# A recurrent gate on one core: the first weight pair's low-rank part ahead of everything, and block 1 spread over more engines

## The chip, the cores and the metric

The kernel runs on one core of a Trainium2 chip. The metric is device time in microseconds. The core has five engines with queues of their own, each worked off in order: TensorE (PE, matmul), VectorE (DVE), ScalarE (ACT), GpSimd (POOL), and SyncE (SP), which here only issues DMAs.

## The reference, cut to what matters

The input is x, 2 x 1024 tokens of 512 features. With xn the layer norm of x, the output is x + s * silu(f). Here f is a gated feed-forward net with low-rank (LoRA) additions, and s is a long convolution whose kernel comes from a small state space model:

```
def _lora_linear(x, w, a, b):
    base = jnp.einsum('bsd,od->bso', x, w)
    low = jnp.einsum('bsr,or->bso', jnp.einsum('bsd,rd->bsr', x, a), b)
    return base + low * SCALING            # SCALING = 2, rank R = 16
h1 = _lora_linear(x, w1, lora_A1, lora_B1)     # 512 -> 1376
h3 = _lora_linear(x, w3, lora_A3, lora_B3)
g = jax.nn.silu(h1) * h3
return _lora_linear(g, w2, lora_A2, lora_B2)   # 1376 -> 512

K = _s4_kernel(Lambda, p, q, B, Ct, step, L)   # L = 512
y = irfft(rfft(u, n=2*L) * rfft(K, n=2*L), n=2*L)[..., :L] + D[0] * u
```

All is float32.

## The kernel before, in words

**Tokens.** The 2048 tokens are four blocks of 512 (`x_in[0]` to `x_in[3]`), each four tiles of 128. Blocks 0 and 1 form the first half of the tokens, 2 and 3 the second. Every tile is normalized: its mean and variance come from VectorE's statistics (`norm_stats`, L246 and L247) or from two accumulating ScalarE passes (`act_sums`, `act_squares`, with GpSimd's `act_means` and `act_variances` behind them). `norm_root` (L280 to L283) turns the variances of a block, or of two, into scale and shift by ten tiny VectorE operations, and `normalize` scales the tiles on ScalarE (L292) and GpSimd (L296). `transpose` has TensorE turn a tile (L303) into one of two PSUM banks, and ScalarE copies it out: block 0 and 2 into `xr` (L311), block 1 and 3 into `b12` and `xr` (L313, L314).

**Weights.** The 1376 hidden features are five pairs of 2 x 128 and a last chunk of 96. A pair's tile `w` has eight slots; w1 and w3, cut in half along the 512 features, fill slots 1 (a11), 2 (a12), 0 (a21) and 3 (a22). The low-rank part is not applied to the tokens but added to the weights: `lora_product` (L381) multiplies the rank-16 factors `lo_d` and `lo_h` into a PSUM bank, and `merge` (L391) has VectorE add twice that onto the loaded weights. `merge_pair` does it for pair 0 in two halves, `merge_whole_pair` for the others, `merge_last` for the last chunk.

**Products.** The feed-forward products are two nested seven-product (Strassen-Winograd) schemes. The outer one works on halves of the features and of the tokens, the inner one on the halves within. So there are sums of tokens (`outer_token_sum` L327, `inner_token_sum` L339 to L345) and of weights (`outer_weight_sums` L439, `inner_weight_sum` L451, `last_sums` L490 to L493 on GpSimd), all additions of whole tiles, most of them on VectorE. A `Chain` is one outer product: seven inner products into the banks x, w and y (L754), with copies by ScalarE (L774 takes a snapshot of x, L792 copies x into the bank w, onto which the next product then adds) and additions by VectorE (L778) that gather them. GpSimd multiplies the gated halves (L835) and adds others (L868).

**Order.** The order on each engine is written by hand. `at(place, what)` puts a piece of work on a heap; the pieces are taken out by place, one unit being roughly one product on TensorE, and each engine executes its instructions in that order. The start (loads, norms of block 0, the last chunk's LoRA) comes ahead of the heap as plain code; the places -11 to 0 are the rest of the ramp; the first heavy products start at -11 (last chunk) and -4 (pair 0).

**Start.** SP issues the loads of x blocks 0 and 1, the last chunk, pair 0, x blocks 2 and 3, and pair 1. ScalarE's queue issues the first LoRA factors. TensorE executes products of the identity with itself (`keep_warm`, L989) until there is work.

**Second half.** From about 285 us on the down projection runs in units of 128 tokens (`unit`), together with the state space model's resolvent, roots and matrix (`s4_work`, L561 to L745), a few small VectorE steps after every turn of a unit. `run` takes one turn of a unit, one of a list of `parts` (the sums of the next group's activations, L1176), and some S4 steps, and so on. `nothing` is an empty part.

Of the kernel before, what the change touches and what calls it, by code (L numbers as in the profile page):

```python
# [107 lines left out]
def s4_gated_ffn(  # L108
# [141 lines left out]
    def act_sums(b, tt):  # L250
        if tt == 0:
            sums_of_x[b] = small.tile([P, 3, NTT], F32, tag="act_sums", name="act_sums")
# [4 lines left out]
    def act_means(b):  # L257
        sums = sums_of_x[b]
        nc.gpsimd.tensor_scalar(sums[:, 1, :], sums[:, 0, :], -1.0 / DIM, None, mult)
        nc.gpsimd.tensor_scalar(norms[b][:, :, 0], sums[:, 0, :], 1.0 / DIM, None, mult)  # L260
# [11 lines left out]
    def act_variances(b):  # L272
        nc.gpsimd.tensor_scalar(
            norms[b][:, :, 1], sums_of_x[b][:, 2, :], 1.0 / DIM, None, mult
        )
# [11 lines left out]
    def normalize(b, on_act=(0, 2)):  # L287
        rstd, shift = norms[b]
        for tt, t in enumerate(x_in[b]):
# [5 lines left out]
            else:  # L295
                nc.gpsimd.tensor_scalar(t, t, rstd[:, one], shift[:, one], mult, add)  # L296

    def transpose(b, tiles, tag="aux"):
        sb, low = divmod(b, 2)
        for tt in tiles:  # L300
# [11 lines left out]
            else:  # L312
                nc.scalar.copy(b12[sb][:, :, at_], halves[:, 0])  # L313
# [80 lines left out]
    def load_pair(c):  # L394
        w = wpool.tile([P, 8, 2, 2, P], F32, tag="w", name="w")
        for v, src in enumerate((w1T, w3T)):
            for half in range(2):
                slot = (1, 2, 0, 3)[2 * v + half]
                rows = src[half * HALF : (half + 1) * HALF, PAIR_AT[c] : PAIR_AT[c] + 2 * P]
                nc.sync.dma_start(  # L400
                    out=w[:, slot].rearrange("p k m h -> p k (m h)"),
                    in_=rows.rearrange("(k p) h -> p k h", p=P),
                )
        return w

    def merge_pair(c, w, half, tag="aux"):

        ps = [bank(tag), bank(tag)]
# [4 lines left out]
        for v in range(2):  # L413
            to = w[:, (1, 2, 0, 3)[2 * v + half]].rearrange("p k m h -> p (k m h)")
            after(1.6 + v, lambda to=to, v=v: merge(to, ps[v]))
# [559 lines left out]
    w_pair, s_pair = {0: load_pair(0)}, {c: {} for c in range(NPAIR)}  # L975
# [22 lines left out]
    primed = bank("w"), bank("w")  # L998
    for ps in primed:
        keep_warm(ps, 12, True)  # L1000
    ps_last = lora_last()
    mv = norm_tile(0)
    norm_stats(0, range(NTT))
    norm_root(mv, 0)
    normalize(0)

    for i in range(2):
        keep_warm(primed[1], (5, 2)[i])
        transpose(0, range(2 * i, 2 * i + 2))
# [3 lines left out]
    norm_stats(1, range(2, NTT))  # L1013
    norm_root(mv, 1)
    merge_last(w_last, ps_last, 1)
# [41 lines left out]
    at(-10, lambda: normalize(1))  # L1057
    at(-9.9, lambda: last_sums(w_last, s_last))
    at(-9, lambda: merge_pair(0, w_pair[0], 0))
    at(-3.8, lambda: merge_pair(0, w_pair[0], 1))  # L1060
    for i in range(2):
        at(-6 + i, lambda i=i: transpose(1, range(2 * i, 2 * i + 2), "y"))
# [529 lines left out]
```

## Time and profile before

| | us |
|---|---|
| median of 3 runs | 445.49 (444.50 to 445.88) |
| the profiled execution | 446.04 |
| its span, first to last instruction | 444.2 |
| PE busy | 437.1 |
| VectorE busy | 318.0 |
| GpSimd busy | 206.1 |
| ScalarE busy | 144.6 |

A line of a timeline gives the start and the length in us, engine, source line, operation, output <- inputs, the shape, the number of instructions, and in brackets idle time ahead and what ended it. A chain of waits is followed back from the last instruction, at each step to what released it. DMA share is the mean busy share of the 16 DMA engines.

### The profile page before, as it was taken

The page shows a single profiled execution, that of the slowest core. Times are in us where ns is not written, and L with a number is a line of the kernel's source. Part 1 is how long each engine was busy: PE and PEld are TensorE (multiplying, and loading weights), DVE is VectorE, ACT ScalarE, POOL GpSimd, SP SyncE. Part 2 cuts the span into 40 slices and gives each one's busy share as a digit, 9 for nine tenths or more (in the row PEclk, how much of TensorE's full clock was granted, in tenths as well). Part 3 has the DMA queues.
Part 4 walks back from the last instruction along what each step waited for, and adds up shares of the span by engine and source line. Part 5 has one row for each costly group of instructions (what it writes and reads, how often), then busy time and mean ns, then how long its engine had stood idle before and what let it go on. Part 6 is the DMA issues. An engine that isn't in the chain of part 4 may idle for free.

```text
span 444.2 us, 5192 instructions
## 1 busy us (share of the span) xinstructions
PE 437.1 (98%) x1722; PEld 271.8 (61%) x1722; DVE 318.0 (72%) x534; ACT 144.6 (33%) x296; POOL 206.1 (46%) x156
## 2 busy tenths in 40 slices
PE   8999999999999999999999999999999999999996
PEld 8645333344444444444443447888888999999995
DVE  5799999955984687468745796979595885653234
ACT  2676332543254325532453242111101212212221
POOL 2306469895669467945794469400000122222221
PEclk9999999999999999999999999999999999999999
DMA  8911304025102500260036526395901843323211
GB/s 263 364 51 38 136 0 147 0 76 174 37 24 72 165 24 24 76 180 25 24 123 209 163 91 213 106 357 187 346 19 72 281 141 96 142 95 96 78 65 48
DMA packets 35466, 53.61 MB, mean 121 GB/s; under 512 B 4688, under 2 KB 21520, under 8 KB 35312
## 3 DMA queue, kind: packets, MB, share of 16 engines
q1 hardware_dynamic: 35312, 53.14, 36.6%
q8 instruction: 13, 0.21, 0.2%
q10 hardware_dynamic: 128, 0.14, 0.1%
q14 instruction: 13, 0.11, 0.1%
HBM read 33.88 MB, written 19.40 MB: 120 GB/s over the span
## 4 chain that ended last, share of the span: by engine, by line
PE 70%; DVE 18%; DMA 7%; issue 2%; ACT 1%; SPq 1%; DVEq 0%; ACTq 0%
PE x L754 35%; PE y L754 18%; PE w L754 9%; PE aux L928 4%; PE w L928 2%; DVE xt L327 2%; DVE s L1176 2%; DVE w L439 1%; DMA t_in<-g_dram 1%; DMA g<-g_dram 1%; DMA t_in<-in_x_dram 1%; DMA lo_h<-in_b1T_dram 1%; DMA w<-in_w1T_dram 1%; DVE t_in L341 1%; DVE s L451 1%
## 5 line engine op out<-in xcount | busy, mean ns | idle before, releaser
L1310 POOL TENSOR_TENSOR o<-o,xin 128x512 f32<-128x512 f32 (+1 forms) x17 | 23.3, 1370 | 134.3 <-DVE o L1309 134.3
L835 POOL TENSOR_TENSOR s<-c,s 128x512 f32<-128x512 f32 (+1 forms) x44 | 63.2, 1441 | 16.5 <-ACT c L827 11.3
L774 ACT COPY s<-x 128x512 f32<-128x512 f32 (+1 forms) x54 | 31.6, 586 | 87.0 <-PE x L754 85.6
L754 PE MATMUL x<-t_in,s 128*128 128x512 f32 (+1 forms) x148 | 55.2, 500 | 0.0
L778 DVE TENSOR_TENSOR s<-s,y 128x512 f32<-128x512 f32 (+1 forms) x54 | 36.1, 679 | 16.4 <-PE y L754 10.9
L868 POOL TENSOR_TENSOR s<-ua_three,s 128x512 f32<-128x512 f32 x20 | 35.9, 1793 | 23.7 <-DVE s L778 23.7
L754 PEld LDWEIGHTS x<-t_in,s 128*128 128x128 f32 x148 | 26.8, 190 | 22.8 <-issue 12.0
L868 POOL TENSOR_TENSOR ua_three<-ua_three,s 128x512 f32<-128x512 f32 x20 | 33.1, 1653 | 14.8 <-DVE s L778 14.8
L754 PE MATMUL y<-t_in,s 128*128 128x256 f32 (+1 forms) x108 | 35.9, 459 | 0.0
L1332 ACT COPY z<-x 128x256 f32<-128x256 f32 x24 | 8.8, 371 | 70.4 <-PE x L754 70.3
L1307 DVE TENSOR_TENSOR aux<-aux,m 128x384 f32<-128x384 f32 x32 | 18.1, 565 | 15.9 <-PE aux L928 14.3
L868 POOL TENSOR_TENSOR s<-u_three,s 128x512 f32<-128x512 f32 x20 | 28.5, 1426 | 1.8 <-ACT c L827 1.0
L827 ACT ACTIVATE c<-c 128x512 f32<-128x512 f32 x40 | 25.2, 632 | 9.6 <-DVE c L868 9.6
L754 PEld LDWEIGHTS y<-t_in,s 128*128 128x128 f32 x108 | 20.1, 190 | 11.3 <-issue 8.8
L792 ACT COPY w<-x 128x512 f32<-128x512 f32 (+1 forms) x37 | 21.1, 570 | 12.5 <-PE x L754 12.4
L754 PE MATMUL x<-t_in,w 128*128 128x512 f32 x40 | 20.9, 603 | 0.0
L754 PE MATMUL x<-xr,w 128*128 128x512 f32 x40 | 20.6, 614 | 0.1
L868 POOL TENSOR_TENSOR u_three<-ua_three,u_three 128x512 f32<-128x512 f32 x10 | 12.7, 1272 | 17.1 <-DVE u_three L778 17.0
L754 PE MATMUL x<-xr,s 128*128 128x512 f32 x40 | 20.6, 616 | 0.1
L754 PE MATMUL x<-xt,w 128*128 128x512 f32 x40 | 20.6, 597 | 0.0
L754 PE MATMUL x<-xt,s 128*128 128x512 f32 x40 | 20.4, 592 | 0.0
L754 PE MATMUL y<-xt,s 128*128 128x512 f32 x40 | 20.0, 597 | 0.4 <-DVE u_three L778 0.4
(302 smaller groups left out, 914.0 us busy)
## 6 DMA issues: line engine op xcount, KB each, us to landing
g_dram<-s SPq DMA_DIRECT2D x40, 256.0 KB, 2.2
g<-g_dram SPq DMA_DIRECT2D x10, 512.0 KB, 5.9
xin<-in_x_dram SPq DMA_DIRECT2D x16, 256.0 KB, 2.8
out_dram<-o SPq DMA_DIRECT2D x14, 256.0 KB, 2.0
t_in<-g_dram SPq DMA_DIRECT2D x6, 512.0 KB, 4.2
w<-in_w1T_dram SPq DMA_DIRECT2D x10, 256.0 KB, 3.3
w<-in_w3T_dram SPq DMA_DIRECT2D x10, 256.0 KB, 4.3
s<-in_x_dram SPq DMA_DIRECT2D x8, 256.0 KB, 4.1
```

The lines of the kernel that those rows point to most:

```text
L327: nc.vector.tensor_tensor(to, a, b, add if name == 2 else sub)
L754: nc.tensor.matmul(ps[:, cols], lhsT=lhsT, rhs=rhs if parts == 1 else rhs[:, cols], start=first and i == 0 and part == 0, stop=i == len(pa ...
L774: nc.scalar.copy(t, self.x)
L778: nc.vector.tensor_tensor(t, t, self.y, add)
L792: nc.scalar.copy(self.w, self.x)
L827: nc.scalar.activation(c, c if src is None else src, AF.Silu)
L835: nc.gpsimd.tensor_tensor(g, act, g, mult)
L868: (nc.vector if o < 20 else nc.gpsimd).tensor_tensor(to, a, b, add)
L928: nc.tensor.matmul(to[:, n * P : (n + 1) * P], lhsT=x_, rhs=by, start=start, stop=True, skip_group_check=True,)
L1176: lambda t=t, op=op: nc.vector.tensor_tensor(*t, op)
L1307: nc.vector.tensor_tensor(y[:, P:], y[:, P:], m[:, n * P : (n + 3) * P], add)
L1310: (nc.vector if last else nc.gpsimd).tensor_tensor(o, o, self.xin[h][:, cols], add)
```

## The change

- Pair 0's LoRA products move from the places -9 and -3.8 to the very start, behind 16 warming products instead of 24. ScalarE multiplies them by two and writes them from PSUM into the pair's (still empty) weight tile (`lora_pair`). The weights themselves are no longer loaded by SP and merged by VectorE: GpSimd issues four DMAs, after its part of block 0's norm, that add the weights from DRAM onto what is in the tile.
- The later warming products (5 and 2, between the transposes) go; two into an aux bank come after the last chunk's LoRA products.
- Block 0's first tile is scaled by VectorE, its third by ScalarE; of block 1, tiles 0 and 3 by VectorE, 1 by ScalarE, 2 by GpSimd. VectorE copies the b12 half of block 1's transposes.
- Block 1's transposes come one place earlier. Of block 2, the first tile's statistics move to ScalarE, the other three on VectorE behind the weight sums.
- The third inner weight sum of each next pair comes 1.2 places later, and in the second half, units 2 and 3, two more empty parts precede the sums of the following group.

```diff
--- before.py
+++ after.py
@@ -248,16 +248,16 @@
 
 
     def act_sums(b, tt):
-        if tt == 0:
+        if b not in sums_of_x:
             sums_of_x[b] = small.tile([P, 3, NTT], F32, tag="act_sums", name="act_sums")
         nc.scalar.activation(
             value("c"), x_in[b][tt], AF.Copy, accum_out=sums_of_x[b][:, 0, tt : tt + 1]
         )
 
-    def act_means(b):
-        sums = sums_of_x[b]
-        nc.gpsimd.tensor_scalar(sums[:, 1, :], sums[:, 0, :], -1.0 / DIM, None, mult)
-        nc.gpsimd.tensor_scalar(norms[b][:, :, 0], sums[:, 0, :], 1.0 / DIM, None, mult)
+    def act_means(b, tiles=slice(0, NTT)):
+        s, neg, _ = (sums_of_x[b][:, i, tiles] for i in range(3))
+        nc.gpsimd.tensor_scalar(neg, s, -1.0 / DIM, None, mult)
+        nc.gpsimd.tensor_scalar(norms[b][:, tiles, 0], s, 1.0 / DIM, None, mult)
 
     def act_squares(b, tt):
         one = slice(tt, tt + 1)
@@ -269,9 +269,9 @@
             accum_out=sums_of_x[b][:, 2, one],
         )
 
-    def act_variances(b):
+    def act_variances(b, tiles=slice(0, NTT)):
         nc.gpsimd.tensor_scalar(
-            norms[b][:, :, 1], sums_of_x[b][:, 2, :], 1.0 / DIM, None, mult
+            norms[b][:, tiles, 1], sums_of_x[b][:, 2, tiles], 1.0 / DIM, None, mult
         )
 
     def norm_root(mv, *blocks):
@@ -284,7 +284,7 @@
         for n, b in enumerate(blocks):
             norms[b] = [t[:, n * NTT : (n + 1) * NTT] for t in (rstd, shift)]
 
-    def normalize(b, on_act=(0, 2)):
+    def normalize(b, on_act=(0, 2), on_vector=()):
         rstd, shift = norms[b]
         for tt, t in enumerate(x_in[b]):
             one = slice(tt, tt + 1)
@@ -293,7 +293,8 @@
                     t, t, AF.Identity, bias=shift[:, one], scale=rstd[:, one]
                 )
             else:
-                nc.gpsimd.tensor_scalar(t, t, rstd[:, one], shift[:, one], mult, add)
+                engine = nc.vector if tt in on_vector else nc.gpsimd
+                engine.tensor_scalar(t, t, rstd[:, one], shift[:, one], mult, add)
 
     def transpose(b, tiles, tag="aux"):
         sb, low = divmod(b, 2)
@@ -310,7 +311,9 @@
             if low == 0:
                 nc.scalar.copy(xr[:, 0:2, sb, :, at_], halves)
             else:
-                nc.scalar.copy(b12[sb][:, :, at_], halves[:, 0])
+                (nc.vector.tensor_copy if sb == 0 else nc.scalar.copy)(
+                    b12[sb][:, :, at_], halves[:, 0]
+                )
                 nc.scalar.copy(xr[:, 2, sb, :, at_], halves[:, 1])
 
     def outer_token_sum(sb, name):
@@ -391,28 +394,34 @@
         nc.vector.scalar_tensor_tensor(to, ps, LORA_SCALE, to, mult, add)
 
 
-    def load_pair(c):
-        w = wpool.tile([P, 8, 2, 2, P], F32, tag="w", name="w")
-        for v, src in enumerate((w1T, w3T)):
-            for half in range(2):
+    def pair_room():
+        return wpool.tile([P, 8, 2, 2, P], F32, tag="w", name="w")
+
+    def load_pair(c, w=None):
+
+        how = (nc.gpsimd.dma_start, {"accum_op": add}) if w is not None else (nc.sync.dma_start, {})
+        w = pair_room() if w is None else w
+        for half in range(2):
+            for v, src in enumerate((w1T, w3T)):
                 slot = (1, 2, 0, 3)[2 * v + half]
                 rows = src[half * HALF : (half + 1) * HALF, PAIR_AT[c] : PAIR_AT[c] + 2 * P]
-                nc.sync.dma_start(
+                how[0](
                     out=w[:, slot].rearrange("p k m h -> p k (m h)"),
                     in_=rows.rearrange("(k p) h -> p k h", p=P),
+                    **how[1],
                 )
         return w
 
-    def merge_pair(c, w, half, tag="aux"):
-
-        ps = [bank(tag), bank(tag)]
+    def lora_pair(c, w, half):
+
+        ps = [bank("x"), bank("w")]
         for k in range(2):
             for v in range(2):
                 n = slice(k * 2 * P, (k + 1) * 2 * P)
                 lora_product(ps[v][:, n], v, 2 * half + k, PAIR_AT[c], 2 * P, k == 0)
         for v in range(2):
             to = w[:, (1, 2, 0, 3)[2 * v + half]].rearrange("p k m h -> p (k m h)")
-            after(1.6 + v, lambda to=to, v=v: merge(to, ps[v]))
+            nc.scalar.mul(to, ps[v], LORA_SCALE)
 
     def merge_whole_pair(c, w, first=None, delays=(1.15, 2.3, 4.3, 4.4)):
 
@@ -972,7 +981,7 @@
     x_in[1] = load_x(1)
     make_upper_triangular(nc, tri, 1.0, diag=True)
     w_last, s_last = load_last()
-    w_pair, s_pair = {0: load_pair(0)}, {c: {} for c in range(NPAIR)}
+    w_pair, s_pair = {0: pair_room()}, {c: {} for c in range(NPAIR)}
     x_in[2], x_in[3] = load_x(2), load_x(3)
     w_pair[1] = load_pair(1)
     for v, f in enumerate(factors):
@@ -995,24 +1004,26 @@
                 skip_group_check=True,
             )
 
-    primed = bank("w"), bank("w")
-    for ps in primed:
-        keep_warm(ps, 12, True)
+    for _ in range(2):
+        keep_warm(bank("w"), 8, True)
+    for half in range(2):
+        lora_pair(0, w_pair[0], half)
     ps_last = lora_last()
+    keep_warm(bank("aux", True), 2, True)
     mv = norm_tile(0)
     norm_stats(0, range(NTT))
     norm_root(mv, 0)
-    normalize(0)
-
+    normalize(0, (2,), (0,))
+    load_pair(0, w_pair[0])
     for i in range(2):
-        keep_warm(primed[1], (5, 2)[i])
         transpose(0, range(2 * i, 2 * i + 2))
     mv = norm_tile(1)
     norm_stats(1, range(2))
     merge_last(w_last, ps_last, 0)
     norm_stats(1, range(2, NTT))
+    merge_last(w_last, ps_last, 1)
     norm_root(mv, 1)
-    merge_last(w_last, ps_last, 1)
+    one = slice(0, 1)
     mv_late = norm_tile(2, 3)
     ab_last = last_operands(w_last, s_last)
 
@@ -1054,23 +1065,26 @@
             if (c, n) == (NPAIR - 1, 5):
                 places = (*PLACES[:-1], (4, 13.5))
             add_chain(2 + 7 * c + n, pair_chain(c, n), places)
-    at(-10, lambda: normalize(1))
-    at(-9.9, lambda: last_sums(w_last, s_last))
-    at(-9, lambda: merge_pair(0, w_pair[0], 0))
-    at(-3.8, lambda: merge_pair(0, w_pair[0], 1))
+    at(-10.8, lambda: normalize(1, (1,), (0, 3)))
+    at(-10.7, lambda: last_sums(w_last, s_last))
     for i in range(2):
-        at(-6 + i, lambda i=i: transpose(1, range(2 * i, 2 * i + 2), "y"))
+        at(-7 + i, lambda i=i: transpose(1, range(2 * i, 2 * i + 2), "y"))
     for n, name in enumerate((3, 2, 1)):
         at((-2.3, -1.5, -1)[n], lambda name=name: outer_token_sum(0, name))
         at(-0.6 + 0.3 * n, lambda name=name: outer_weight_sums(w_pair[0], (name,)))
     at(0.4, lambda: outer_token_sum(0, 4))
     at(0.8, lambda: outer_weight_sums(w_pair[0], (4,)))
     for tt in range(NTT):
-        at(-6 + 0.8 * tt, lambda tt=tt: norm_stats(2, (tt,)))
+        if tt > 0:
+            at((0.9, 0.92, 0.95)[tt - 1], lambda tt=tt: norm_stats(2, (tt,)))
         at(-1.4 + 0.1 * tt, lambda tt=tt: act_sums(3, tt))
         at((-0.3, -0.2, 1.7, 1.8)[tt], lambda tt=tt: act_squares(3, tt))
     at(-0.9, lambda: act_means(3))
     at(1.9, lambda: act_variances(3))
+    at(-0.8, lambda: act_sums(2, 0))
+    at(-0.7, lambda: act_means(2, one))
+    at(2, lambda: act_squares(2, 0))
+    at(2.1, lambda: act_variances(2, one))
     at(6.9, lambda: norm_root(mv_late, 2, 3))
     at(7.3, lambda: normalize(2))
     at(7.4, lambda: normalize(3, (0,)))
@@ -1127,7 +1141,7 @@
                     lambda nx=nx, name=name: outer_weight_sums(w_pair[nx], (name,)),
                 )
             for name, when in (
-                (3, ready(7)),
+                (3, ready(7) + 1.2),
                 (1, ready(5)),
                 (2, ready(5) + 4),
                 (4, max(ready(3), ready(5) + 8)),
@@ -1492,7 +1506,7 @@
     hold(HOLD)
     run(
         [unit(2, read), unit(3, read)],
-        [*nothing * 2, *more],
+        [*nothing * 4, *more],
         8,
     )
     for _ in s4_work:
```

## The prediction

> **What bounds the kernel now.** I read the page's busy times first, then the matmul timeline of the start, then the chain that ended last, then the waits of TensorE.
>
> The page, busy time by engine:
>
> ```profile
> PE 437.1 (98%) x1722; PEld 271.8 (61%) x1722; DVE 318.0 (72%) x534; ACT 144.6 (33%) x296; POOL 206.1 (46%) x156
> ```
>
> TensorE has hardly a hole, so time can come from two places only: matmuls that needn't be there, and the few holes. The timeline of PE (start, length, line, tiles, records; every matmul here is two records) shows the start:
>
> ```profile
> 1.37 8.52 PE L989 MATMUL w<-ident 128*128 128x128 f32 x48 [1.37 <-POOL ident masks.py:199]
> 9.82 1.13 PE L381 MATMUL y<-lo_h,lo_d 16*128 16x96 f32 x16
> 10.88 1.38 PE L989 MATMUL w<-ident 128*128 128x128 f32 x10
> 12.10 1.04 PE L303 MATMUL aux<-ident,s 128*128 128x128 f32 x8
> ...
> 14.42 1.94 PE L754 MATMUL x<-xr,last 128*96 128x256 f32 x8
> 16.30 1.13 PE L381 MATMUL aux<-lo_h,lo_d 16*128 16x256 f32 x8
> 17.36 1.96 PE L754 MATMUL w<-xr,last 128*96 128x512 f32 x4
> ```
>
> L989 is the warming product; the first useful work of the dense stretch starts at 12.10. The chain of waits (start, length, what) says who sets the end:
>
> ```profile
> 31.22 0.09 DVE veps L280
> ...
> 33.15 2.22 ACT t_in L292 x3
> 35.37 0.48 ACT ua_three L774
> 35.85 0.03 issue
> 35.87 0.69 DVE ua_three L778
> ...
> 70.24 0.61 DVE ua_one L868
> 70.85 0.04 issue
> 70.89 1.13 PE x L754 x2
> ```
>
> From 70.89 on the chain is TensorE. Before that it is VectorE: the root of the late norms (L280 to L283), ScalarE's three scalings behind it, and from 35.87 VectorE without a gap. So up to 70.89 TensorE is nearly, not quite, the bound: its own shift counts only as far as VectorE shifts too. Two holes lie later. At 82.20 TensorE waits for a total that VectorE has queued behind a 2.15 us weight sum (timelines of DVE, then PE):
>
> ```profile
> 79.40 2.15 DVE L451 TENSOR_TENSOR s<-w 128x896 f32<-128x896 f32 x1
> 81.48 0.67 DVE L778 TENSOR_TENSOR u_three<-u_three,y 128x512 f32<-128x512 f32 x1
> ```
>
> ```profile
> 82.20 1.13 PE L754 MATMUL y<-xt,s 128*128 128x512 f32 x2 [0.35 <-DVE u_three L778]
> ...
> 331.72 0.49 PE L709 MATMUL aux<-room 128*128 128x128 f32 x2 [0.66 <-DVE room L690]
> ```
>
> and the second, at 331.72, goes back to VectorE standing 4.20 us behind a load:
>
> ```profile
> 317.13 0.96 DVE L1176 TENSOR_TENSOR s<-t_in 128x768 f32<-128x768 f32 x1 [4.20 <-DMA t_in<-g_dram]
> ```
>
> **TensorE's start, part by part.** Warming products fall from 24 + 5 + 2 to 16 + 2. The first 28 records start every 0.213 us (until 7.3), later ones every 0.109, so the 32 that stay end at 7.7. The pair's LoRA products follow: two sets of four at 1.06 (16.30 to 17.36), to 9.8; the last chunk's 16 records at 1.05, to 10.85; two warming products 0.44, to 11.3. The factors landed by 6.44 and cost no wait. Block 0's tile is scaled by VectorE from 9.7 in 0.48 (its one 128x512 TENSOR_SCALAR form, L571) and ready at 10.2. So the transposes start at 11.3, not 12.10. The third needs ScalarE's copy of the first (two aux banks), now without warming products to fill the time, so the lead stays about 0.9: L754 x<-xr,last at 13.5, ending at 15.4.
>
> Now a wait is added. The product w<-xr,last adds onto a bank that ScalarE copies first; at 16.40 that copy took 0.56 and hid under the LoRA products (1.06) that are moved away. It is bare now: 0.7 us idle, w<-xr,last at 16.1 instead of 17.36 (1.3 earlier), ending at 17.9. Block 1's transposes follow if scaled. VectorE: one scaling 0.5, four statistics at 0.82, two merges at 0.47, a root at 1.96, from 9.7: shift ready at 16.4 (15.37 before), its two tiles at 16.9 and 17.4; ScalarE's tile at 17.2, behind its copy; GpSimd's at 17.2. All before use, so transposes run 17.9 to 19.9 (two y banks; each is copied out by VectorE and ScalarE in parallel, 0.42 the longer) and the first pair product starts at 19.9 instead of 21.55. The second LoRA set (1.06 at 22.51) is gone as well; after a 0.45 wait for the first token sum TensorE leads by about 2.4 at w<-xr,w.
>
> **VectorE's share of it.** Before, its first token sum began at 22.59; now block 1 is copied out at 20.5, 2.05 earlier. From there to the late root it loses two merges at 0.6 (the first two lay in a gap) and gains three statistics at 0.82 that lay in a gap before: 2.05 + 1.2 - 2.45 = 0.8. ScalarE's extra sum and square of one tile (0.61 + 0.72, less four copies at 0.27) and GpSimd's small follower end at about 29.5, before VectorE's 30.4, and so cost nothing. The root, the scalings and ua_three then come 0.8 earlier: TensorE, 2.7 early by then (0.3 more from a start at 28.23 that stood behind a weight sum, which now comes in time), stands about 2 us at what was 35.89, and 0.8 is what is left of its lead. From 35.87 to 70.85 no work of VectorE is removed; 0.8 is carried through.
>
> **GpSimd's transfers.** No transfer of GpSimd and none that adds is in this trace. What is queued behind them on GpSimd: block 1's third tile (used at 19.0, so free by 18.2), then last_sums (first used at 21.2). GpSimd is free at 11.3, so four issues may take 1.7 us each. From below: an issue costs SP 0.42 to 0.51 for the same shape, and no gain below that is possible, since it has no such work now. From above: GpSimd's longest instruction here is 5.12 (L868), four of which would end at 31.8 and put all of it 13 us late. I take about 1 us, nearer to the issues of the same shape, which hold no arithmetic. Landing: a21 is needed at 24.2 by the weight sums, a22 at 24.8, a11 at 19.9. Below: the same 256 KB took 4.8 from issue (6.95) to landing (11.76), the next three 0.74 apart, in a stretch where the DMA share is already 1.07; so 17 to 19. Above: double bytes for reading the target and a half share of the engines against the x loads, 4 x 0.74 apart, give 17 + 3 x 3 = 26, 1.2 late for a22. I take no lateness. SP drops four issues (2.0 us), so x2 and x3 are issued earlier and share the engines; they were needed no sooner than 21.
>
> [...]
>
> **Later edits.** The third inner weight sum comes 1.2 units later: for pair 1 it falls behind u_three, which is then done at 80.1 instead of 82.07. The excess of that matmul start over its pitch is 0.51; I take 0.5. For later pairs there is no hole at this place, so nothing. Two more empty turns before group 2's sums: 16 small S4 steps run in the 4.20 us hole, two sums (0.96 + 0.95) leave the stretch before L690; z comes some 2.8 us earlier, against an excess of 0.82 + 0.16 at 331 to 332: 0.95. Those sums are then due two turns before they are used, still in time at 349.
>
> **Sum.** 0.8 + 0.5 + 0.95 = 2.25. The profiled execution took 446.04 (span 444.2 and 1.8 around it), 0.55 above the median; its holes are taken to be the median run's, so 445.49 - 2.25 = 443.2.
>
> **Rivals.** (a) Issuing is dear: 2 us each keep GpSimd until 19.3, the third tile comes at 20.1 instead of 19.0, and all behind it 1.1 later: 444.3; at 2.5 each 446.3. For it: GpSimd stretches to three times its usual 1.65 beside VectorE. Against: few two-input VectorE operations run from 11 to 17. (b) Slower: the adding transfers land late, because they don't overlap. Four at 4.8 each, from 11.3, end at 30.5; a22 is then 5.7 late, VectorE's in-order queue stands there, and the root with it: 443.2 + 5.7 = 448.9. It decides from a landing 2.25 late (27.1), and can be told from 28.4. For it: a read, an addition and a write on one place. Against: the plain loads overlap to 0.74. (c) More gain: the VectorE operations beside GpSimd's (L451 took 1.08 to 2.15) fall apart in the new phase, or the root is not what holds ScalarE; 1 us more: 442.2.
>
> **Numbers.** Forecast 0.50; (a) 0.20, (b) 0.18, (c) 0.12. This kernel's measurement tells 0.3% (1.34 us) from no change: faster below 444.15, slower above 446.83. Forecast and (c) are faster, with a little of (a): 0.64. Most of (a) is same: 0.15. (b) and the dear end of (a): 0.21. The range 441.7 to 447.6 takes in (c), its further half us, (a), and the milder half of (b).
>
> **What would show it.** Right: first transposes near 11.3, first pair product near 20, a PE hole of about 2 us before what was 35.89, no hole at 82 and 331, VectorE's 4.2 us hole shrunk. Wrong: GpSimd's third tile after 18.2, weight sums (L439) waiting on a DMA, a root later than 31.1, or slow matmul records after the hole.

## The result

| | median of runs, us | lowest to highest | runs | ratio to before, 95% interval |
|---|---|---|---|---|
| before | 445.17 | 444.50 to 445.88 | 6 | |
| changed | 447.38 | 446.99 to 448.07 | 6 | 1.0050 [1.0034, 1.0065] |

The change makes the kernel 2.2 us slower; the forecast was 2.25 us faster. The profiled execution of the changed kernel took 448.07 us, its span 446.3 us. Six later runs of the same kernel gave a median of 447.66 us (1.0060 [1.0048, 1.0073]).

### The profile after

The code has moved by a few lines: the product L754 is L763, the copies L313 and L314 are L314 and L317, the weight sums L439 are L448, the merge L391 is L394, the scaling L296 is L297, the load is L408. From the page of the changed kernel, the busy times, the granted clock by slices, and the queue that GpSimd feeds:

```profile
PE 435.8 (98%) x1696; PEld 270.9 (61%) x1696; DVE 316.1 (71%) x535; ACT 145.4 (33%) x298; POOL 212.2 (48%) x162
...
PEclk9898999999999999999999999999999999999999
...
q0 software_dynamic: 1088, 1.05, 1.5%
```

TensorE is busy 1.3 us less, and the kernel takes longer. In the second and the fourth of the 40 slices (11 to 22 and 33 to 45 us) the granted clock is below full. The timeline of PE in the changed kernel says where:

```profile
1.38 6.74 PE L998 MATMUL w<-ident 128*128 128x128 f32 x32 [1.38 <-POOL ident masks.py:199]
...
9.87 1.03 PE L384 MATMUL y<-lo_h,lo_d 16*128 16x96 f32 x16
10.83 1.20 PE L998 MATMUL aux<-ident 128*128 128x128 f32 x4
12.09 3.36 PE L304 MATMUL aux<-ident,s 128*128 128x128 f32 x16
15.29 1.94 PE L763 MATMUL x<-xr,last 128*96 128x256 f32 x8
17.93 1.96 PE L763 MATMUL w<-xr,last 128*96 128x512 f32 x4 [0.71 <-ACT w L801]
19.73 1.04 PE L304 MATMUL y<-ident,s 128*128 128x128 f32 x8
21.34 1.06 PE L304 MATMUL y<-ident,s 128*128 128x128 f32 x8 [0.58 <-ACT xr L317]
22.24 1.02 PE L763 MATMUL x<-xr,w 128*128 128x512 f32 x2
...
38.08 1.99 PE L763 MATMUL x<-xr,w 128*128 128x512 f32 x2 [2.15 <-ACT ua_three L783]
39.86 2.76 PE L763 MATMUL y<-xt,last 128*96 128x512 f32 x4
```

The two last warming products start at 10.83, as planned (10.85). Then the sixteen records of block 0's transposes take 3.36 us where before two sets of eight took 1.04 and 1.16. The late product, the x<-xr,w that waits for ScalarE's snapshot of x (at 35.89 before), stands at 38.08, and its two records take 1.99 where they took 1.12. Busy times by windows show the granted clock (the column PEclk, third from the end) behind both:

```profile
11.00:14.00 3.00, 2.94 (x13) 2.42 (x14) 2.86 (x9) 1.55 (x3) 3.00 (x5) 0.50 1.05 389
...
38.00:42.00 4.00, 3.92 (x5) 1.46 (x6) 3.90 (x5) 1.10 (x3) 2.34 (x3) 0.57 0.18 47
```

The trace has half the clock from 10.89 to 14.31 and from 38.20 to 41.61, each 3.41 us long, from here on called a half-clock window. VectorE's and then GpSimd's timeline of the changed kernel, in the stretch that sets the late product:

```profile
23.30 1.29 DVE L330 TENSOR_TENSOR xt<-xr,b 128x512 f32<-128x512 f32 x2 [0.44 <-ACT xr L317]
...
30.66 0.69 DVE L246 BATCH_NORM_STATS2 stats<-t_in 128x6 f32<-128x512 f32 x1
...
33.26 0.17 DVE L280 TENSOR_SCALAR veps<-mv 128x8 f32<-128x8 f32 x1
```

```profile
11.74 1.34 POOL L408 DMA_DIRECT2D w<-in_w1T_dram  x1
12.70 1.63 POOL L408 DMA_DIRECT2D w<-in_w3T_dram  x1
13.44 2.13 POOL L408 DMA_DIRECT2D w<-in_w1T_dram  x1
14.16 2.63 POOL L408 DMA_DIRECT2D w<-in_w3T_dram  x1
17.00 1.02 POOL L297 TENSOR_SCALAR s<-s,rs_y,shift 128x512 f32<-128x512 f32 x1 [0.21 <-DVE shift L283]
```

The root (the 128x8 veps) comes at 33.26; before it came at 31.14, and 30.4 was forecast. The late product is 2.19 us behind before, instead of 0.8 ahead. The four transfers landed at 20.8, 22.4, 25.3 and 26.4, not at 17 to 19. Further on, matched one by one, the matmuls stand behind before by 3.88 us after the second half-clock window, 2.78 at before's 82.20 (the hole there is gone), 3.75 at its 107.87 (a new hole), 3.53 at 302.6, and 2.30 from 340 on (the hole at 331 is gone too).

### The profile page after: what moved, and what is told of

Its sections match the earlier page's. It is cut to its first block, busy times and chain, and to the rows that moved or that the text cites. A ratio compares the mean times of both kernels' runs of the same rounds, so it can differ in the third digit from the quotient of the medians.

```text
span 446.3 us, 5145 instructions
## 1 busy us (share of the span) xinstructions
PE 435.8 (98%) x1696; PEld 270.9 (61%) x1696; DVE 316.1 (71%) x535; ACT 145.4 (33%) x298; POOL 212.2 (48%) x162
## 4 chain that ended last, share of the span: by engine, by line
PE 85%; POOL 6%; DVE 4%; issue 2%; ACT 1%; DMA 1%; SPq 0%; POOLq 0%; DVEq 0%; ACTq 0%
PE x L763 41%; PE y L763 21%; PE w L763 11%; PE aux L937 4%; PE w L937 2%; POOL ua_three L877 2%; POOL s L877 2%; PE aux L304 2%; PE w L998 2%; POOL s L844 1%; DVE xt L330 1%; DMA w<-in_w1T_dram 1%; PE y L384 1%; POOL u_three L877 1%; PE y L536 1%
## 5 line engine op out<-in xcount | busy, mean ns | idle before, releaser
L844 POOL TENSOR_TENSOR s<-c,s 128x512 f32<-128x512 f32 (+1 forms) x44 | 62.5, 1427 | 18.8 <-ACT c L836 13.3
L763 PE MATMUL x<-t_in,s 128*128 128x512 f32 (+1 forms) x148 | 55.2, 500 | 0.0
L877 POOL TENSOR_TENSOR s<-ua_three,s 128x512 f32<-128x512 f32 x20 | 32.3, 1617 | 28.5 <-DVE s L787 28.5
L763 PEld LDWEIGHTS x<-t_in,s 128*128 128x128 f32 x148 | 26.8, 190 | 22.8 <-issue 12.5
L763 PE MATMUL y<-t_in,s 128*128 128x256 f32 (+1 forms) x108 | 35.9, 459 | 0.9 <-DVE w L394 0.9
L763 PEld LDWEIGHTS y<-t_in,s 128*128 128x128 f32 x108 | 20.1, 190 | 12.4 <-issue 8.4
L763 PE MATMUL x<-xr,w 128*128 128x512 f32 x40 | 21.5, 636 | 2.2 <-ACT ua_three L783 2.2
L877 POOL TENSOR_TENSOR u_three<-ua_three,u_three 128x512 f32<-128x512 f32 x10 | 15.6, 1558 | 12.4 <-DVE u_three L787 12.3
L763 PE MATMUL x<-t_in,w 128*128 128x512 f32 x40 | 20.8, 603 | 0.0
L763 PE MATMUL x<-xt,w 128*128 128x512 f32 x40 | 20.6, 597 | 0.0
L763 PE MATMUL x<-xr,s 128*128 128x512 f32 x40 | 20.4, 613 | 0.0
L763 PE MATMUL x<-xt,s 128*128 128x512 f32 x40 | 20.4, 592 | 0.0
L763 PE MATMUL y<-xt,s 128*128 128x512 f32 x40 | 19.8, 593 | 0.0
```

The source lines that it names most:

```text
L763: nc.tensor.matmul(ps[:, cols], lhsT=lhsT, rhs=rhs if parts == 1 else rhs[:, cols], start=first and i == 0 and part == 0, stop=i == len(pa ...
L844: nc.gpsimd.tensor_tensor(g, act, g, mult)
L877: (nc.vector if o < 20 else nc.gpsimd).tensor_tensor(to, a, b, add)
```

## The experiments

Every ratio is to runs of the kernel before on the same chip at the same time, so versions from different chips are compared by their ratios. Each version builds on the one above it, unless its text says otherwise.

### The changed kernel once more

> The changed kernel once more. Its first profile shows two windows of 3.41 us in which the granted clock is 0.5, one behind the LoRA products of the start and one behind the hole before 38.08, while the other five runs report a clock of 1.000. Theory (several terms: late root, late loads of pair 2, and the clock only now and then): 1.9 to 2.3 us above the kernel before also without half-clock windows; a profile without them starts its first w<-xr,last near 16.1 and still has the hole before x<-xr,w. Rival (the clock is the cause): without half-clock windows the time is that of the kernel before, within 0.5 us.

Measured: 447.66 us (446.91 to 448.35, 6 runs). This profile has no half-clock window at the start (only one from 39.46 to 42.87, behind the hole), so it shows what else delays the root. Timeline of DVE, then of PE, in this run:

```profile
20.97 1.29 DVE L330 TENSOR_TENSOR xt<-xr,b 128x512 f32<-128x512 f32 x2 [0.44 <-ACT xr L317]
...
27.72 1.29 DVE L448 TENSOR_TENSOR w<-w 128x512 f32<-128x512 f32 x2 [2.44 <-DMA w<-in_w3T_dram]
...
33.33 0.17 DVE L280 TENSOR_SCALAR veps<-mv 128x8 f32<-128x8 f32 x1
```

```profile
20.24 1.12 PE L763 MATMUL x<-xr,w 128*128 128x512 f32 x2 [0.17 <-DMA w<-in_w1T_dram]
21.81 1.93 PE L763 MATMUL y<-xt,last 128*96 128x512 f32 x4 [0.44 <-DVE xt L330]
25.32 1.10 PE L763 MATMUL w<-xr,w 128*128 128x512 f32 x2 [1.58 <-DMA w<-in_w1T_dram]
```

VectorE starts 2.33 us earlier than in the other profile and reaches the root at the same time, because it stands 2.44 us for a22, which landed at 27.62. TensorE stands 1.58 for a12. So two delays of nearly one length lie side by side: either the clock makes VectorE late, or the landing does. That fits the runs of the changed kernel, which all lie within 1.5 us whatever their clock. Five of the first six and one of these report a mean clock of 1.000; they took 446.99 to 447.83, at least 1.8 above before. So the loss doesn't need a half-clock window, and the rival falls.

### SP's loads in the old order

The diff also turned the loop of `load_pair` (halves outside, w1 and w3 inside), for the pairs that SP loads too. Here those have the old order again.

```diff
-        for half in range(2):
-            for v, src in enumerate((w1T, w3T)):
+        places_ = [(v, half) for half in range(2) for v in range(2)]
+        for v, half in places_ if how[1] else sorted(places_):
+            src = (w1T, w3T)[v]
```

> The changed kernel with one thing undone: pairs 1 to 4, which SP loads, are loaded in the old order (both halves of w1, then both of w3). Theory: the new order brings the second half of w1, which the first merge of pair 2 needs, as the third transfer, behind a store; landing 2.3 us later, VectorE's 3.54 us wait at the first L394 and TensorE's 0.92 us hole at 111.62 follow. Undone: no hole there, 0.9 to 1.1 us less than the changed kernel. Rival (the later inner weight sum holds the merges): the hole stays, change under 0.2.

Measured: 446.30 us (445.11 to 448.50, 12 runs), ratio 1.0033 [1.0017, 1.0050]. VectorE's timeline, first of the changed kernel, then of this one, where pair 2 is merged:

```profile
110.87 0.69 DVE L394 SCALAR_TENSOR_TENSOR w<-y,w 128x512 f32<-128x512 f32 x1 [3.54 <-DMA w<-in_w1T_dram]
```

```profile
107.17 0.69 DVE L394 SCALAR_TENSOR_TENSOR w<-y,w 128x512 f32<-128x512 f32 x1 [0.90 <-DMA w<-in_w1T_dram]
```

The first merge takes both halves of w1. With w3's first half in between, the second half landed at 110.75 (before: 105.76), VectorE waited, and TensorE had a new hole of 0.92 before the product at 111.6. It is gone here. In medians that is 1.1 to 1.4 us, a little more than expected; among runs with a mean clock of 0.998 or more it is about 2 (445.1 to 446.0 against 447.0 to 447.8). The forecast didn't have this term at all.

### Block 1's copies on ScalarE again

```diff
-                (nc.vector.tensor_copy if sb == 0 else nc.scalar.copy)(
-                    b12[sb][:, :, at_], halves[:, 0]
-                )
+                nc.scalar.copy(b12[sb][:, :, at_], halves[:, 0])
```

> As a_order, and ScalarE copies the b12 half of block 1's transposes again, as in the kernel before. Theory: with two engines the two copies of one bank run one after the other (VectorE 0.43, then ScalarE 0.38: 0.81 a tile), with ScalarE alone 0.27 each, 0.53 a tile; the second pair of transposes and the first token sum come 0.4 to 0.6 earlier, the root as much, 0.3 to 0.6 us less than a_order. Rival (GpSimd's transfers, landed at 20.8, 22.4, 25.3 and 26.4, set the pace): within 0.2 of a_order, with waits of L448 or of w<-xr,w on those transfers.

Measured: 446.21 us (444.82 to 447.12, 11 runs), 1.0028 [1.0018, 1.0038]; against the one above nothing that can be told; the 0.3 to 0.6 expected doesn't show. In the changed kernel ScalarE's copy waits for VectorE's copy of the same bank (0.43, then 0.38 us: 0.81 per tile), where the forecast had them side by side (0.42); ScalarE alone does both in 0.53. The stall of the second transposes (0.58 at 21.34) is 0.35 in the versions with this edit. In this profile VectorE still stands 1.8 us for a22 behind it, as the rival had it.

### Three statistics back into VectorE's gap

```diff
-            at((0.9, 0.92, 0.95)[tt - 1], lambda tt=tt: norm_stats(2, (tt,)))
+            at(-10.5, lambda tt=tt: norm_stats(2, (tt,)))
```

> As a_order_copies, and VectorE's three statistics of block 2 stand ahead of block 1's transposes (in its gap) instead of behind the fourth weight sum. Theory: they cost 2.45 us of the path to the late root; taken off it, the hole before x<-xr,w (2.3 us) goes, the root starts 1.5 to 2.4 earlier, and the time is 1.3 to 2.3 us below a_order_copies, that is 0.5 to 2 us below the kernel before. Rival (GpSimd's transfers set the pace): the weight sums then wait for the transfer of a22, the root comes at most 0.8 earlier, and the time stays within 0.8 of a_order_copies.

Measured: 444.97 us (444.24 to 446.35, 11 runs), 0.9999 [0.9989, 1.0009]: 1.2 us, just under what was expected and half of the 2.45 that the three cost on VectorE's path. In the profile the landing takes the rest: VectorE still waits 2.37 us for a22 (27.75 in this run) and TensorE 1.6 for a12.

### Pair 1's loads held back as well

SP issues pair 1's loads only behind VectorE's first token sum, so that nothing large shares the DMA engines with GpSimd's transfers.

```diff
-    w_pair[1] = load_pair(1)
+    w_pair[1] = pair_room()
...
+    def held_load():
+        nc.vector.memset(w_pair[1][:, 0:4, 0, 0, 0:1], 0.0)
+        load_pair(1, w_pair[1])
+    at(-2.2, held_load)
```

> As a_order_copies_stats, and SP issues pair 1's four loads only after VectorE's first token sum (a memset of four columns of their tile holds them), so that GpSimd's adding transfers have the DMA engines to themselves. Theory (the adding transfers land late because their packets take 101 ns instead of 48 and take turns with pair 1's): they start near 16.3 as before, but a22 lands near 23 instead of 27.7; the 2.37 us wait of L448 and the 1.6 us wait of w<-xr,w go, the root starts 0.5 to 2 earlier, time 0.7 to 2 us below a_order_copies_stats and below the kernel before. Rival (a fixed time per adding transfer, whatever else runs): a22 stays past 26, time within 0.4 of a_order_copies_stats.

Measured: 442.30 us (441.87 to 444.03, 6 runs), 0.9943 [0.9927, 0.9958]; this version is faster than both kernels, and 2.7 us faster than the one above, more than expected. The transfers' rows (engine, operation, count, KB each, median us from issue to landing), of the changed kernel and then of this one:

```profile
w<-in_w1T_dram POOLq DMA_DIRECT2D x2, 256.0 KB, 10.5
...
w<-in_w3T_dram POOLq DMA_DIRECT2D x2, 256.0 KB, 11.0
```

```profile
w<-in_w1T_dram POOLq DMA_DIRECT2D x2, 256.0 KB, 8.2
w<-in_w3T_dram POOLq DMA_DIRECT2D x2, 256.0 KB, 8.6
```

They landed at 19.4, 20.7, 22.0 and 23.4, and nobody waits for them. Repeated beside later versions:

> The version with four repairs (loads in the old order, ScalarE's copies, three statistics in VectorE's gap, pair 1's loads held back) once more, beside the others of this call: 442.3, 0.9943 of before, and 1 us below the kernel before with the later sums alone (443.26). If the 1 us was chance, it comes out at 443 or above.

Measured: 442.41 us (441.96 to 444.27, 10 runs), 0.9950 [0.9936, 0.9964].

### The hold alone

The same hold, in the changed kernel with nothing else altered.

> The changed kernel with one thing altered: SP's loads of pair 1 wait until VectorE has made its first token sum (four columns of the tile are zeroed behind it), so that GpSimd's adding transfers have the DMA engines to themselves. Load order, block 1's copies and the place of block 2's statistics stay as in the changed kernel. Theory (the adding transfers are slow because pair 1's loads take every other packet): they land near 19.5, 20.7, 22 and 23.4 as in the version that held these loads with the other three repairs, VectorE's weight sums wait for no DMA, and the time falls by 1.5 to 2.5 us from 447.5: 445 to 446. Rival (the landing was no bound of its own; whatever binds next, the statistics on VectorE's path or ScalarE's copies, holds the root at the same time): 447 to 447.7.

Measured: 446.42 us (444.85 to 446.99, 10 runs), 1.0027 [1.0012, 1.0043], a gain of 1.0 to 1.2 in medians (1.0 to 1.5 by the ratios, as this is another chip), less than expected. VectorE's root and TensorE's late product:

```profile
31.12 0.17 DVE L280 TENSOR_SCALAR veps<-mv 128x8 f32<-128x8 f32 x1
```

```profile
35.93 2.01 PE L763 MATMUL x<-xr,w 128*128 128x512 f32 x2 [2.16 <-ACT ua_three L783]
```

No weight sum waits for a DMA, the root comes at 31.12 instead of 33.33, and the late product is 0.04 behind before instead of 2.19. But TensorE, which now leads, has its hole all the same, and it loses 1.7 us in the half-clock window behind it; the new hole of the load order (0.99 at 109.55) is there too. The four runs with a mean clock of 0.998 took 444.9 to 445.3, the six with 0.994 to 0.996 took 446.3 to 447.0. Against the six runs of the changed kernel at 1.000 (447.0 to 447.8) the four are 2.2 us faster, of which 0.2 can be the chip's: without a half-clock window the whole delay of the root is regained.

### The hold, and the hole filled

Eight products of the identity, which nothing uses, ahead of the late product.

```diff
+    at(9, lambda: keep_warm(psum.tile([P, 512], F32, tag="w0", name="w", bufs=1), 8, True))
```

> The changed kernel with pair 1's loads held back (446.42) and one more thing: eight products of the identity with itself (1.75 us at the full clock, used by nothing) stand ahead of the product x<-xr,w that waits for ScalarE's snapshot, in the hole of 2.16 us; they go into a bank that VectorE frees at 33.7, as the hole begins, so they delay nothing. Theory (the hole costs more than its length, since TensorE's clock is granted by half for one window of 3.41 us behind it): no half-clock window after the hole, the records of x<-xr,w and y<-xt,last at 427 ns instead of 853, and the median falls to that of the undisturbed runs of the version without the filling, 445.1 (444.85 to 445.33). Rival (the half-clock windows have nothing to do with the hole, or the root alone sets the time): 446.4 as without, with half-clock windows near 36 in some runs.

Measured: 445.76 us (444.41 to 448.05, 12 runs), 1.0022 [1.0005, 1.0039]. By windows, with the granted clock third from the end, without the filling and with it:

```profile
36.00:39.40 3.40, 3.40 (x4) 1.21 (x5) 3.37 (x5) 0.95 (x2) 2.19 (x3) 0.50 0.09 23
```

```profile
36.00:39.40 3.40, 3.30 (x19) 2.41 (x20) 2.40 (x5) 2.67 (x6) 3.40 (x6) 1.00 0.01 2
```

These two executions don't have the same course, as this one has a half-clock window at the start (10.94 to 14.35). The changed kernel's first profile does: there the late product stood at 38.08 behind 2.15 us of hole, and took 1.99. Here, the hole filled:

```profile
35.93 2.05 PE L998 MATMUL w<-ident 128*128 128x128 f32 x16
38.09 1.12 PE L763 MATMUL x<-xr,w 128*128 128x512 f32 x2
39.05 1.88 PE L763 MATMUL y<-xt,last 128*96 128x512 f32 x4
```

The full clock was first granted at 7.48 there and at 7.53 here, so the 3.41 us windows lie alike, and only the unfilled hole is followed by half clock. Runs with a mean clock of 0.996 or less are two of twelve instead of six of ten. So by this pair the hole is the cause of that window. In time little shows: 0.7 us in medians, but on another chip, where before takes 444.63 instead of 444.92; by the ratios it is 0.2 us, the intervals overlap, and 1.3 was expected. The ten runs with a mean clock of 0.998 or more still lie between 444.4 and 446.9, so something else moves them, and the hole's price in the median isn't settled.

### GpSimd's transfers without the addition

Built on the version with the three statistics moved. Same place and order, but the transfers only copy; pair 0's low-rank part is lost.

```diff
-        how = (nc.gpsimd.dma_start, {"accum_op": add}) if w is not None else (nc.sync.dma_start, {})
+        how = (nc.gpsimd.dma_start, {}) if w is not None else (nc.sync.dma_start, {})
```

> As a_order_copies_stats, with GpSimd's transfers at the same place but plain: they overwrite, so pair 0's LoRA part is lost. Theory (adding doubles the packet): its packets take about 50 to 60 ns instead of 101, a22 lands near 22 to 24, the wait of L448 (2.37) is under 0.5, time 0.7 to 2 us lower than a_order_copies_stats. Rival (the path of GpSimd itself is slow, not the adding): packets and landings stay within 10% of those with adding, and so does the time.

Measured: 444.27 us (442.80 to 446.01, 12 runs), 0.9978 [0.9962, 0.9993]. GpSimd's timeline, and its queue on the page:

```profile
11.66 0.92 POOL L408 DMA_DIRECT2D w<-in_w1T_dram  x1
12.59 0.73 POOL L408 DMA_DIRECT2D w<-in_w3T_dram  x1
13.31 0.72 POOL L408 DMA_DIRECT2D w<-in_w1T_dram  x1
14.03 0.72 POOL L408 DMA_DIRECT2D w<-in_w3T_dram  x1
```

```profile
q0 software_dynamic: 320, 1.05, 0.7%
```

A plain transfer went in 64 packets of 4 KB, 189 ns each beside other loads; an adding one in 256 packets of 1 KB, 101 ns each: per byte 2.1 times the time on the engines. The theory had a wrong packet (50 to 60 ns), and the factor of two right. The plain ones landed at 17.7, 18.8, 21.2 and 22.1, and pair 1's loads end after them (24.95). So the addition, in that packet form, makes the last landing 5.7 us later (27.75 against 22.05); with plain transfers VectorE and TensorE no longer wait for any. The median is 0.7 us lower, the least that was expected: the six runs with a mean clock of 0.998 or more took 442.8 to 443.7, the six with 0.994 to 0.996 took 444.9 to 446.0.

### Plain transfers first of all

They are issued at the very start, ScalarE's scalings into the tile are left out, and pair 0's low-rank part is lost.

```diff
+    load_pair(0, w_pair[0])
     x_in[2], x_in[3] = load_x(2), load_x(3)
...
-            nc.scalar.mul(to, ps[v], LORA_SCALE)
+            pass
```

> As a_order_copies_stats, but GpSimd's four loads of pair 0 are plain, the first of its work after the identity, and ScalarE's four scalings are left out, so the first pair has no LoRA part. It shows two things. First, what the change is worth when no landing binds: theory, 1 to 2.4 us below a_order_copies_stats. Second, when a transfer of GpSimd starts: issued at about 2 us into the running x loads, its first packet comes 3 to 4 us after the first issue ends if that time is the issue's own, and only after x has landed (near 16) if the x loads in front of it are what held it in the changed kernel.

Measured: 444.40 us (443.63 to 445.61, 12 runs), 0.9986 [0.9975, 0.9996], 0.6 us below the version with the statistics moved, less than the 1 to 2.4 expected. The first packet flowed at 5.0, 3.3 us after the first issue began (2.3 after its end, where 3 to 4 were expected) and long before x had landed: most of the time to the first packet doesn't come from the x loads in front of it. The transfers landed at 7.6, 8.4, 10.0 and 11.2, far ahead of use, and take their share from block 0's and 1's loads instead: block 1's last tile landed at 12.6 instead of 9.5, and the transposes waited 1.1 us for block 0's first scaled tile.

### The later sums alone

The kernel before with the change's last two edits, and nothing of its start.

```diff
-                (3, ready(7)),
+                (3, ready(7) + 1.2),
...
-        [*nothing * 2, *more],
+        [*nothing * 4, *more],
```

> The kernel before with the two later sums alone: the third inner weight sum 1.2 places later, two more empty parts in units 2 and 3. The prediction gave 0.5 + 0.95 us for them. Theory: the holes at 82.20 and 331.72 go and the time is 1.0 to 1.5 us less than before. Rival (the later weight sum delays the merges of pair 2 behind it): the first goes and a hole near 108 comes, 0 to 0.9 us less.

Measured: 443.26 us (442.85 to 444.49, 6 runs), 0.9961 [0.9947, 0.9975]: 1.86 us less than before, more than was expected, where the forecast's two terms make 1.45. The product that waited at 82.20, in this profile:

```profile
80.24 1.88 PE L754 MATMUL y<-xt,s 128*128 128x512 f32 x4
```

It waits for nothing, and neither the holes at 82 and 331 nor a new one near 108 are there. So these edits were right, and if the parts add, the rest of the diff costs 447.4 - 443.3 = 4.1 us.

### Do matmuls of 16 rows keep the clock up?

In the kernel before, the filling products take 16 rows of the identity instead of 128.

```diff
-                lhsT=ident,
-                rhs=ident,
+                lhsT=ident[:R, :],
+                rhs=ident[:R, :],
```

> The kernel before; the products that fill TensorE's start take only the first 16 rows of the identity (same columns, same count; their results are used by nothing). Theory (matmuls of 16 rows do not hold the clock up): records of the filling products stay near 213 ns apart all the way, none at 109, the first transposes come 2 to 3 us later than the 12.1 of before and run at half clock, and the granted clock is 0.5 up to there. Rival (any matmul counts as work): spacing falls to 109 ns between 4.9 and 7.5 us as before, and the transposes start near 12.

Measured: 453.13 us in a single run, span 451.4. The timeline of PE:

```profile
1.37 10.39 PE L989 MATMUL w<-ident 16*128 16x128 f32 x47 [1.37 <-POOL ident masks.py:199]
...
15.74 1.97 PE L303 MATMUL aux<-ident,s 128*128 128x128 f32 x8
...
20.55 3.34 PE L754 MATMUL x<-xr,last 128*96 128x256 f32 x8
...
24.88 1.96 PE L754 MATMUL w<-xr,last 128*96 128x512 f32 x4
```

Records stay 213 ns apart, at half speed, though TensorE is never idle. From 15.74 on there are transposes of 128 rows, with 16-row products between them once more (17.64 to 18.79); the trace's first record of the full clock is at 23.48 (ahead of its first record a view prints 1.00), after a window of 3.41 us that held nothing but matmuls of 128 rows. The transposes come 3.6 us later than before, more than expected. So 16-row products did not raise the clock here, and in the changed kernel's first profile 2.8 us of the pair's moved products, ahead of the transposes, were followed by half clock (from 10.89).

### The fourth statistic back on VectorE too

In the version with the hold and the three other repairs, the two ScalarE passes over block 2's first tile are replaced by VectorE's statistics again.

```diff
-    at(-0.8, lambda: act_sums(2, 0))
-    at(-0.7, lambda: act_means(2, one))
-    at(2, lambda: act_squares(2, 0))
-    at(2.1, lambda: act_variances(2, one))
+        at(-10.5, lambda tt=tt: norm_stats(2, (tt,)))
```

> The version with the loads in the old order, ScalarE's copies, the three statistics of block 2 in VectorE's gap and pair 1's loads held back; now the fourth statistic of block 2 goes back to VectorE too, instead of two passes on ScalarE. In that version's trace the late root waits 1.37 us for GpSimd's last variance, at 29.64. Theory (ScalarE's extra sum and square, put down as free in the prediction, now set the root): VectorE reaches the root 0.8 later (28.9), ScalarE's last square ends 0.9 earlier, the root starts near 29.0 and the time falls by 0.6 us, 441.7 against 442.3. Rival (the gap was not spare, VectorE's token sums come 0.8 later and pass it on): 442.3 to 443.1.

Measured: 441.67 us (441.44 to 442.60, 6 runs), 0.9933 [0.9918, 0.9949], the fastest version. The root on VectorE, with the hold and then in this version:

```profile
29.64 0.17 DVE L280 TENSOR_SCALAR veps<-mv 128x8 f32<-128x8 f32 x1 [1.37 <-POOL mv L273]
```

```profile
29.17 0.17 DVE L280 TENSOR_SCALAR veps<-mv 128x8 f32<-128x8 f32 x1 [0.44 <-POOL mv L273]
```

With the landing repaired and the three statistics moved, ScalarE's extra sum and square had become what the root waits for. The gain is 0.6 to 0.7, as expected; the intervals of the two versions overlap.

## Why the prediction was wrong, point by point

The forecast was 2.25 us faster, the kernel is 2.2 slower. Two steps failed. The adding transfers were taken to land by 19 and to hold nobody up; they landed at 20.8 to 27.6, and the root came at 33.3 instead of 30.4. And the order of SP's loads had no term at all.

**Landing of the adding transfers (17 to 19, "no lateness").** This is the term that failed most. The forecast took its lower bound, from plain loads of SP. The two sizes in its upper bound, double work and a half share, were near: per byte an adding packet took 2.1 times a plain one, and the queue of pair 1's loads moved about as many packets beside them. That the doubling comes from reading the target isn't shown. The bound itself (26) was too low for undisturbed starts: 27.6 and 27.75. The parts, as measured in the repeated run: the first packet flows at 16.3, 4.8 us after GpSimd starts to issue; then 1024 packets of 101 ns, 6.5 us of all 16 engines; and pair 1's loads took as many packets (119 of each queue in the microsecond from 19; 115 and 111 in the first profile), so about 11 us for both. The forecast expected x2 and x3 to come earlier and share the engines. They had landed by 16.5; it was pair 1's loads, issued from 11.7 instead of 14.7, that shared. This is rival (b) at a smaller size: its 30.5 was too dark, its place (VectorE's weight sums standing for a22, the root behind them) was right. The deadline of a12 on TensorE (about 23.7 in an undisturbed start) was not in the text.

**What was left out: the order of SP's loads.** A term of nothing where 1.1 to 1.4 us were due in medians. Every load of pairs 1 to 4 changed its place in a queue, and the first merge of a pair needs the first and the third of the new order.

**TensorE's start.** In the first profile right up to 10.85, and in both in the bare copy (0.71 for 0.7). Wrong at the transposes: 11.3 was forecast, 12.09 at half the clock in the first profile, and 10.57 in the repeated run, where the full clock came at 5.33 instead of 7.48. The warning on slow records was put at the hole at 36; the same risk at 10.9 was missed, where 2.8 us of 16-row products replace warming products. The forecast's 7.3, up to which it takes slow warming records, is one draw: the full clock came 2.15 us apart in the two profiles of the changed kernel.

**Block 1's copies.** Forecast "in parallel, 0.42 the longer", measured in series, 0.81 a tile.

**VectorE's share.** Token sum to root was to take 8.55 - 1.2 + 2.45 = 9.8 us; it took 9.96 in the first profile, and 9.92 and a wait of 2.44 in the repeated run. This term was right, the statistics' cost included. ScalarE's passes were free only while VectorE was later: with the landing repaired and the three statistics moved they hold the root by 1.37.

**The 2 us hole.** Forecast about 2, measured 2.15 to 2.73. Its place was right, but the forecast put no price on the clock behind it. In the first profile records behind it ran at 853 ns instead of 427 and cost 1.7 us: a window of 3.41 us with 2.15 us of hole in it was followed by one at half clock, and so it was in the repeated run (2.1 us in the window) and in the hold alone (2.16).

**Later edits.** Right: no hole at 82 or 331, and 1.86 us alone for 1.45.

**GpSimd's issuing.** Spaced 0.72 to 0.96 apart, from 11.74 to 16.79, so 1.26 us each where about 1 was taken and 1.7 allowed; the third tile came at 17.00, in time, and rival (a) falls. Rival (c) had its half us in the later edits, and nothing else of it showed.

**The sum.** From 447.5 by medians: load order 1.2, copies 0.1, landing 2.7 (beside the others, from 444.97 to 442.30) make 443.5 if the statistics stay where the change put them; the forecast was 443.2. This is worked out, not shown: no run repairs the order and the landing without the statistics. The steps don't add freely either, as the hold alone gives 1.0 to 1.2 in medians and 2.2 only where no half-clock window falls.

## What to carry to other kernels

Price a transfer by its packets (how large, how long each, which other queue moves packets beside it: here 1 KB, 101 ns, and pair 1's loads) and by the time to its first packet (4.8 us here), not by the landing of a plain load of the same size; and hold loads that aren't due out of the way of those that are. When a diff turns a loop, follow every user of that loop, the ones outside the change's purpose too. Where two delays of one length lie side by side, repair both before judging either, and count a hole in TensorE, or a stretch of thin matmuls, with the half clock that can follow it (1.7 us here).

## What the runs showed of the hardware

- In one run with 16-row filling products, 47 records of them in a row, without idle time, stayed 213 ns apart, and the full clock came only at 23.48 us, after a window of 3.41 us with 128-row work alone.
- In the traces the granted clock changed only in steps of 3.41 us, counted from the first full clock, which came at 7.48 us in the changed kernel's first profile, at 5.33 in the repeated run and at 7.53 with the hole filled. Three windows with 2.1 to 2.2 us idle (first profile, repeated run, hold alone) were followed by one at half clock, and so were two with 2.8 us of 16-row products (first profile, hole filled). In the repeated run, where the windows lie 2.15 us earlier, none at half clock followed the same products; and a hole of 2.26 us in the version with block 1's copies on ScalarE had full-speed records behind it (1.12 us for two). The author takes it from this that the phase decides whether one and the same hole is cut in two. Runs of one kernel differ with the clock: with plain transfers, those with a mean of 0.998 or more took 442.8 to 443.7 us, those with 0.994 to 0.996 took 444.9 to 446.0.
- An adding transfer of 256 KB by GpSimd went in 256 packets of 1 KB at 101 ns, a plain one in 64 of 4 KB at 189 ns. The adding instructions took 1.34 to 2.63 us on GpSimd, the plain ones 0.72 to 0.92, though both started 0.72 to 0.96 apart.
- GpSimd's first packet came 4.8 us after its first issue began in both profiles of the changed kernel, and 3.3 us where it issues at the start of the kernel.
- Four adding transfers without pair 1's loads beside them landed 1.3 to 1.4 us apart; beside those loads, in the first profile, 1.1 to 2.9.
